# Attention and FFN on one core: the order of two kinds of exp on ScalarE, of the logs on VectorE, and of PSUM evictions

## The chip, the cores and the metric

The kernel runs on one core of a Trainium2 chip. The metric is the device time of one execution in microseconds (us), the median of several runs. A profile is one further execution, recorded by the hardware. The engines are written PE (TensorE, matmul), PEld (its weight loads), DVE (VectorE), ACT (ScalarE), POOL (GpSimd) and SP (SyncE, which issues DMAs). Each engine works through its own queue in order; engines wait for each other through semaphores.

## The reference

Sixteen sequences of 512 rows and 128 columns are layer-normalised. Sixteen causal heads (key width 8, value width 64) and a gated FFN both start from the normalised rows, and both are added to the input:

```python
def _L0_attn_ref(x, Wq, Wk, Wv, Wo):
    HEADS, D_MODEL, D_V = (16, 128, 64)
    ...
    scores = jnp.einsum('bhqd,bhkd->bhqk', q, k) / scale
    scores = jnp.where(causal, jnp.asarray(-jnp.inf, scores.dtype), scores)
    attn = jax.nn.softmax(scores, axis=-1)
    ctx = jnp.einsum('bhqk,bhkd->bhqd', attn, v)
    ...
    return out @ Wo

# FFN: r = sigmoid(xr @ W_r.T); k = square(relu(xk @ W_k.T)); r * (k @ W_v.T)
x = L0_attn_x
xn = _layernorm(x, axis=-1)
x = x + _L0_attn_ref(xn, ...) + _L0_ffn_ref(xn, ...)
```

All of it is in float32.

## The kernel before

**Two passes over the scores.** Every score is computed twice. The first pass is row-major: `rowscores` (L328) writes queries on partitions and keys along the row into a PSUM tile `sm`, `rowmask` (L341) adds the causal mask with four more matmuls, `rowmax` (L359) takes the negated row maximum on DVE into `negm`, and `rowsum` (L378) runs an exp on ACT, in place, one per head and block, whose accumulator is the row's sum. An ACT exp with an accumulator is two instructions in the trace: the ACTIVATE and an ACTIVATION_READ_ACCUMULATOR behind it; the end of the second is what others wait for. From maximum and sum, `log_sums` (L389, a Ln on ACT) and `sub_logs` (L394, one small subtraction on DVE) make minus the maximum minus the log of the sum, `turn_stats` (L398) transposes it on PE into a tile `pm` and copies it out in two halves on DVE (`mh`, `ml`), and `put_stats` (L409) writes it by DMA from POOL as two more rows of the query operand. The second pass is key-major: `scores` (L424) writes keys on partitions into a PSUM tile `sT`; because of the added rows these scores are already normalised, and `weights` (L435) takes one exp of 128x1024 from `sT` into `e`, the attention weights, and zeroes the triangle on POOL. `weigh` (L447) multiplies `e` by the values into `av`, `take_ctx` (L462) evicts `av` on DVE, `project_out` (L468) does the last product into `po`.

**Units.** Two head pairs of one sequence make a group of five units, so that a sequence (a batch in the code) has 20 units and the whole run 320. This text calls the place of a unit in its group its kind, 0 to 4, and its place in the sequence its position, 0 to 19. `ROWS` and `KEYS` (L301 to L315) say what a unit holds: `rowsum` has four exps in kinds 0, 2 (384, 384, 128 and 128 columns) and 4 (four of 256), and two of 512 in kinds 1 and 3. `weights` is one exp of 128x1024 in each.

**What sets the order.** Nothing is scheduled automatically: the wrapper `_InOrder` (L33) keeps every engine's queue in the order in which the Python code issues, so all instructions carry its line, 42, in the trace, and are told apart by their tiles. `unit_work(n)` (L531) issues one step of a software pipeline: row scores, mask and maximum for unit n+11, row exps for unit n+10 (`LEAD`), key-major scores and weights for unit n. Per engine, one step is therefore:

- PE: row scores of n+11, key-major scores of n, mask of n+11, then the pieces (projections, FFN) and `weigh`; in a step of kind 1 `weigh` comes ahead of the pieces. In a step of kind 0 the transpose `pm` comes last.
- ACT: the row exps of n+10, in kind 4 the Ln, then the key-major exp of n, then the FFN's exp in position 1.
- DVE: in kinds 0 and 2 `take_ctx`, then `rowmax`, then the pieces' evictions. In kind 0 `sub_logs` is the last piece, and the two small copies of `pm` follow.

**Buffers.** `sm` has two PSUM buffers, so the row scores of n+11 go where those of n+9 were, and PE waits for the last accumulator read of `rowsum` in step n-1. `sT` has one buffer, so the key-major scores of step n wait for the key-major exp of step n-1. `av` has one. All small products (`pv`, `pr`, `pq`, `pk`, `pkv`, `po`, `pm`) share one PSUM tile `m` once the pipeline runs (`m_tile`, L150), so each waits until DVE has evicted the one before. `at(n, ...)` (L492) puts pieces on a step; L504 to L507 place `ffn_sig` (a reciprocal of 128x128 on DVE) and `project_v` (a product and its eviction); both fall on positions 13 and 18 (in the first sequence 13, 14 and 18).

Of the kernel before, what the change touches and what calls it, by code (L numbers as in the profile page):

```python
# [12 lines left out]
AF = mybir.ActivationFunctionType  # L13
# [4 lines left out]
P = 128  # L18
# [29 lines left out]
def attn_ffn_kernel(  # L48
# [48 lines left out]
    pe, dve, act = _InOrder(tc, nc.tensor), _InOrder(tc, nc.vector), _InOrder(tc, nc.scalar)  # L97
# [11 lines left out]
    for name, w in (("wq", Wq), ("wk", Wk)):  # L109
        t = one.tile([P, H * DK], FP, tag=f"{name}_n", name=f"{name}_n")  # L110
# [5 lines left out]
    for i, w in enumerate((W_r, W_k, W_v)):  # L116
        t = one.tile([P, D], FP, tag=f"ffn_n{i}", name=f"ffn_n{i}")
# [172 lines left out]
    def ffn_out(b):  # L290
# [10 lines left out]
    ROWS = (  # L301
        ((0, 2, 0), (0, 0, 384)),
        ((0, 3, 0),),
        ((1, 2, 0), (1, 0, 384)),
        ((1, 3, 0),),
        ((0, 1, 0), (1, 1, 256)),
    )
# [11 lines left out]
    def unit_of(n):  # L319

        n, t = divmod(n, UNITS)
        b, g = divmod(n, NPAIR // 2)
        return (b, g, t) if 0 <= b < B else None
# [4 lines left out]
    def rowscores(b, g, t):  # L328
        q, k = qs[b % 2], ks[b % 2]
        sm = sms[b, g, t] = ps_sm.tile([P, 2, 512], FP, tag="sm", name=f"sm_{b}_{g}_{t}")  # L330
        for w, i, to in ROWS[t]:
            n = (i + 1) * P
            for u in range(2):
                s = slice(64 * u, 64 * u + RS)

                pe.matmul(
                    sm[:, u, to : to + n], q[s, 2 * g + w, i * P : n], k[s, 2 * g + w, :n],
                    start=(to == 0), stop=False,
                )

    def rowmask(b, g, t):  # L341

        ends = [to + (i + 1) * P for _, i, to in ROWS[t]]
        step = ends[-1] - ends[0] or P
        for c in range(2):
            for u in range(2):
                s = slice(64 * u, 64 * u + 64)
                cols = sms[b, g, t][:, u, ends[0] - P :]
                if len(ends) > 1 and step > P:
                    cols = cols.rearrange("q (m k) -> q m k", k=P)[:, 0 :: step // P, 64 * c :]  # L350
                else:
                    cols = cols.rearrange("q (m k) -> q m k", k=P)[:, :, 64 * c :]
                pe.matmul(
                    cols, id64[s, c, :],
                    mask64[s, c : c + 1, 64 * c :].to_broadcast([64, len(ends), P - 64 * c]),
                    start=False, stop=(c == 1),
                )
# [17 lines left out]
                negm[:, :, w, i], sm[:, :, to : to + (i + 1) * P], AX.X, ALU.max, negate=True  # L375
            )

    def rowsum(b, g, t):  # L378
        negm, z = stats[b, g]
        sm = sms.pop((b, g, t))  # L380
        for w, i, to in ROWS[t]:
            for u in range(2):
                cols = sm[:, u, to : to + (i + 1) * P]
                act.activation(
                    cols, cols, AF.Exp,
                    bias=negm[:, u, w, i : i + 1], accum_out=z[:, u, w, i : i + 1],
                )

    def log_sums(b, g):  # L389
        lz = stat.tile([P, 2, 2, NB], FP, tag="lz", name=f"lz_{b}_{g}")  # L390
# [3 lines left out]
    def sub_logs(b, g):  # L394
        negm, z, lz = stats[b, g]
        dve.tensor_tensor(lz, negm, lz, ALU.subtract)
# [12 lines left out]
    def put_stats(b, g):  # L409

        for n, half in enumerate(stats.pop((b, g))):
            for u in range(2):
                r = 64 * u + RS + n
                pool.dma_start(
                    out=qs[b % 2].bitcast(FP)[r : r + 1, 2 * g : 2 * g + 2, :].rearrange(
                        "o p (i t) -> o (p i) t", t=P
                    ),
                    in_=half.bitcast(FP)[2 * NB * u : 2 * NB * u + 2 * NB],
                )
# [4 lines left out]
    def scores(b, g, t):  # L424
        q, k = qs[b % 2], ks[b % 2]
        st = sts[b, g, t] = ps_st.tile([P, 2, 512], FP, tag="sT", name=f"sT_{b}_{g}_{t}")
        for w, j, to in KEYS[t]:
            for u in range(2):
                s = slice(64 * u, 64 * u + RA)
                pe.matmul(  # L430
                    st[:, u, to : to + T - j * P], k[s, 2 * g + w, j * P : (j + 1) * P],
                    q[s, 2 * g + w, j * P : T], start=(to == 0), stop=(to + T - j * P == 512),
                )

    def weights(b, g, t):  # L435
        e = ep.tile([P, 2, 512], FP, tag="e", name=f"e_{b}_{g}_{t}")
        act.activation(e, sts.pop((b, g, t)), AF.Exp)
        for w, j, to in KEYS[t]:

            diag = e[:, :, to : to + P]  # L440
            pool.affine_select(
                out=diag, in_=diag, compare_op=ALU.is_ge, fill=0.0, base=0,
                pattern=[[0, 2], [1, P]], channel_multiplier=-1,
            )
            es[b, 2 * g + w, j] = e[:, :, to : to + T - j * P]
# [16 lines left out]
    def take_ctx(b, p):  # L462
        c = ctxp.tile([P, T], FP, tag="ctx", name=f"ctx_{b}_{p}")
        dve.tensor_copy(c, avs.pop((b, p)))
        ctxs[b, p] = c
# [21 lines left out]

    todo, turns, puts = {}, {}, {}  # L490

    def at(n, f, *args):  # L492
        todo.setdefault(n, []).append((f, args))
# [4 lines left out]
    for b in range(B):  # L498
        n0 = b * per
        if b + 1 < B:  # L500
            r = 0 if b else 7
            at(n0 + r, ffn_r, b + 1)
            at(n0 + r + 1, ffn_exp, b + 1)
            for c, n in enumerate((3, 8, 13, 18) if b else (11, 13, 14, 18)):  # L504
                at(n0 + n, ffn_sig, b + 1, c)
            for m, n in enumerate((1 if b else 3, 5, 12, 13, 14, 16, 17, 18)):
                at(n0 + n, project_v, b + 1, m // 2, m % 2)  # L507
            at(n0 + 7, mix_prev, b + 1, 1)
            at(n0 + 9, mix, b + 1, 1)
            at(n0 + 11, ffn_k, b + 1)  # L510
            at(n0 + 19, ffn_out, b + 1)
            for m, n in enumerate((-1, -1, 0, 0, 4, 4, 5, 5) if b else (0, 0, 0, 0, 4, 4, 5, 5)):
                at(n0 + n, spread_qk, b + 1, *SPREAD[m], slice(0, NPAIR // 2))
            for m, n in enumerate((8, 9, 9, 10, 10, 14, 14, 15)):
                at(n0 + n, spread_qk, b + 1, *SPREAD[m], slice(NPAIR // 2, NPAIR))
        if b + 2 < B:
            at(n0 + 4, deviation, b + 2)
            for c in range(NB):
                at(n0 + (1, 1, 3, 3)[c], row_moments, b + 2, c)
                at(n0 + 4 + c // 2, normalise, b + 2, c)  # L520
            at(n0 + 6, transpose_xn, b + 2)
            at(n0 + 10, project_qk, b + 2, False)
            at(n0 + 15, project_qk, b + 2, True)
            at(n0 + 12, mix_prev, b + 2, 0)
            at(n0 + 14, mix, b + 2, 0)
        for p, n in enumerate((2, 3, 3, 4, 7, 8, 8, 9) if b < B - 1 else (-8, -7, -7, -6, -3, -2, 0, 3)):
            at(n0 + per + n, project_out, b, p)
        if b + 3 < B:
            at(n0 + 11, load_x, b + 3)

    def unit_work(n):  # L531
        now, stat_now, stat_next = (unit_of(n + m) for m in (0, LEAD, LEAD + 1))
        if n in puts:
            put_stats(*puts.pop(n))

        if stat_next:
            rowscores(*stat_next)
        if now:
            scores(*now)
        if stat_next:  # L540
            rowmask(*stat_next)
        t = n % UNITS
        done = {0: (n - UNITS, 0), 2: (n - UNITS, 1)}.get(t)
        if done and unit_of(done[0]):
            b, g, _ = unit_of(done[0])
            take_ctx(b, 2 * g + done[1])
        if stat_next:
            rowmax(*stat_next)

        if stat_now:  # L550
            rowsum(*stat_now)
            b, g, kind = stat_now
            if kind == UNITS - 1:
                log_sums(b, g)
                at(n + 1, sub_logs, b, g)
                turns[n + 1] = puts[n + 2] = b, g
        if now:
            weights(*now)
        pieces = todo.pop(n, ())
        if t != 1:  # L560
            for f, args in pieces:
                f(*args)
        since, w, blocks = WEIGHED[t]
        if unit_of(n - since):
            b, g, _ = unit_of(n - since)
            for j in blocks:
                weigh(b, 2 * g + w, j, (t, j) in ((1, 3), (4, 3)))
        if t == 1:
            for f, args in pieces:
                f(*args)  # L570
        if n in turns:
            turn_stats(*turns.pop(n))
# [41 lines left out]
    for u in range(2):  # L614
        half = slice(64 * u, 64 * u + 64)
        for c in range(2):
            cols = slice(64 * c, 64 * c + 64)
# [81 lines left out]
```

## Time and profile before

| what | value |
|---|---|
| median of three runs | 1032.33 us (1031.92 to 1036.72) |
| the profiled execution, its own time | 1032.25 us |
| its span, first to last instruction | 1030.5 us |
| PE busy | 961.6 us (93%) |
| PE weight loads busy | 525.6 us (51%) |
| ACT busy | 923.9 us (90%) |
| DVE busy | 792.8 us (77%) |
| POOL busy | 520.3 us (50%) |
| row exps, 1024 of them, and their accumulator reads | 513.1 + 201.1 us |
| key-major exps, 320 | 324.3 us |
| mean granted PE clock | 0.979 |

The profiled execution lies 0.08 us under the median, so its rows can be read as the median's. Between about 61 us and 980 us the run repeats a sequence's 20 units about every 60.7 us; before lies the loading and the first ten units' row statistics, behind it the last units' key-major work.

How to read the views quoted below. The page's busy line gives busy microseconds, share of the span and number of instructions of each engine. The chain of waits is the work that ended last, followed back to what released it. A line of a stretch gives, after its start and end, its length and each engine's busy time, then the granted PE clock, the DMA share and GB/s. A line of the waits names who waited for whom, then the total in us, the number of times and the longest. A line of the timeline gives start and length in us, the engine, the operation, output and input tile, shapes and count, and in brackets the idle time ahead of it and who ended that.

### The profile page before, as it was taken

The numbers are of one execution on the slowest core, as the hardware profiler recorded it, in microseconds if no ns is written. First come the engines' busy times: TensorE is split into PE (matmuls) and PEld (weight loads), VectorE is DVE, ScalarE is ACT, GpSimd is POOL, SyncE is SP. The second block draws the span as 40 slices with busy tenths as digits, with TensorE's granted clock in tenths as the row PEclk, the third lists the DMA queues.
The fourth block names the chain that finished last, engine by engine and source line by source line (L and its number), as shares of the span: only waits on it lengthen the run. The fifth ranks groups of instructions, "written<-read, shape, count | busy, mean of one in ns | idle before, by whom it ended". The sixth has DMA issues, their size and how long they took to land.

```text
span 1030.5 us, 24120 instructions
## 1 busy us (share of the span) xinstructions
PE 961.6 (93%) x8771; PEld 525.6 (51%) x8771; DVE 792.8 (77%) x1316; ACT 923.9 (90%) x2449; POOL 520.3 (50%) x957
## 2 busy tenths in 40 slices
PE   3888999999999999999999999999999999999997
PEld 1334454545546464554645555464555646455454
DVE  4877878787787878788788877878878787877741
ACT  0788999999999999999999999999999999999982
POOL 4156454644646464464655546464464546444432
PEclk8679999999999999999999999999999999999999
DMA  7811515225250532625053252504425140433000
GB/s 193 147 23 44 104 25 104 32 67 90 54 104 10 108 42 53 105 54 99 8 109 49 54 105 53 94 14 100 57 54 95 34 97 4 98 49 49 3 13 11
DMA packets 59973, 67.19 MB, mean 65 GB/s; under 512 B 12928, under 2 KB 33024, under 8 KB 59856
## 3 DMA queue, kind: packets, MB, share of 16 engines
q1 hardware_dynamic: 48688, 61.89, 32.1%
q0 software_dynamic: 8640, 1.34, 1.0%
q10 hardware_dynamic: 2528, 2.43, 0.8%
q8 instruction: 70, 1.15, 0.5%
q14 instruction: 47, 0.39, 0.2%
HBM read 39.13 MB, written 25.17 MB: 62 GB/s over the span
## 4 chain that ended last, share of the span: by engine, by line
PE 57%; ACT 19%; DVE 17%; issue 6%; POOL 1%; DMA 0%; ACTq 0%; DVEq 0%; POOLq 0%
PE av L42 16%; ACT sm L42 13%; PE sm L42 12%; PE po L42 10%; DVE negm L42 7%; PE sT L42 7%; ACT e L42 6%; PE pv L42 6%; DVE sig L42 2%; PE pr L42 1%; DVE v L42 1%; PE pm L42 1%; PE pkv L42 1%; DVE xmix L42 1%; PE xnTp L42 1%
## 5 line engine op out<-in xcount | busy, mean ns | idle before, releaser
L42 ACT ACTIVATE sm<-sm,negm 128x384 f32<-128x384 f32 (+3 forms) x1024 | 513.1, 501 | 71.9 <-DMA q<-qh 25.4
L42 DVE TENSOR_REDUCE negm<-sm 128x2 f32<-128x768 f32 (+3 forms) x448 | 398.9, 915 | 125.4 <-PE sm L42 125.1
L42 POOL TENSOR_SCALAR_AFFINE_SELECT e<-e 128x256 f32<-128x256 f32 x512 | 208.2, 426 | 418.2 <-ACT e L42 416.0
L42 ACT ACTIVATE e<-sT 128x1024 f32<-128x1024 f32 x320 | 324.3, 1013 | 21.7 <-PE sT L42 21.7
L42 PE MATMUL av<-e,v 128*64 128x512 f32 (+3 forms) x2048 | 336.2, 439 | 1.3 <-POOL e L42 0.7
L42 PEld LDWEIGHTS av<-e,v 128*64 128x64 f32 x2048 | 138.1, 137 | 166.5 <-issue 139.2
L42 ACT ACTIVATION_READ_ACCUMULATOR sm<-sm,negm 128x1 f32 x1024 | 201.1, 196 | 0.0
L42 PE MATMUL sm<-k,q 33*128 33x384 f32 (+3 forms) x1024 | 163.7, 377 | 4.3 <-ACT sm L42 4.3
L42 PEld LDWEIGHTS sm<-k,q 33*128 33x128 f32 x1024 | 82.9, 188 | 149.0 <-ACT sm L42 72.7
L42 PE MATMUL sT<-q,k 35*128 35x512 f32 (+3 forms) x1024 | 146.5, 338 | 4.5 <-ACT e L42 4.3
L42 PE MATMUL pv<-wv,xnT 128*64 128x512 f32 x512 | 141.5, 632 | 6.9 <-DVE v L42 5.3
L42 PE MATMUL po<-wo,ctx 128*64 128x128 f32 x2048 | 133.2, 277 | 2.1 <-DVE ctx L42 1.6
L42 PEld LDWEIGHTS po<-wo,ctx 128*64 128x64 f32 x2048 | 109.8, 137 | 17.1 <-issue 9.7
L42 PEld LDWEIGHTS sT<-q,k 35*128 35x128 f32 x1024 | 90.2, 187 | 28.6 <-ACT e L42 22.6
L42 PE MATMUL sm<-mask,id 64*128 64x128 bf16 (+2 forms) x1280 | 103.0, 236 | 0.0
L42 DVE COPY v<-pv 128x512 f32<-128x512 f32 x128 | 85.9, 671 | 19.0 <-PE pv L42 18.9
L42 DVE COPY ctx<-av 128x512 f32<-128x512 f32 x128 | 87.3, 682 | 15.6 <-PE av L42 15.5
L42 POOL DMA_DIRECT2D q<-mh x128 | 69.8, 548 | 48.7 <-DVE mh L42 40.7
L42 POOL DMA_DIRECT2D q<-ml x128 | 65.9, 519 | 0.3 <-issue 0.3
L42 DVE RECIPROCAL sig<-e_sig 128x128 f32<-128x128 f32 x64 | 60.2, 941 | 0.0
L42 POOL TENSOR_SCALAR prev<-xnT,omm 128x512 f32<-128x512 f32 x32 | 50.0, 1563 | 12.8 <-DVE xmix L42 12.8
L42 PEld LDWEIGHTS <-id 64*128 64x128 bf16 x1280 | 40.1, 97 | 29.6 <-issue 15.7
(65 smaller groups left out, 568.4 us busy)
## 6 DMA issues: line engine op xcount, KB each, us to landing
q<-q SPq DMA_DIRECT2D x124, 128.0 KB, 4.9
k<-k SPq DMA_DIRECT2D x124, 128.0 KB, 5.5
k<-kh SPq DMA_DIRECT2D x30, 256.0 KB, 2.6
x<-in_L_attn_x_dram SPq DMA_DIRECT2D x16, 256.0 KB, 3.2
q<-qh SPq DMA_DIRECT2D x16, 256.0 KB, 4.2
q<-ql SPq DMA_DIRECT2D x16, 256.0 KB, 4.1
out_dram<-o SPq DMA_DIRECT2D x16, 256.0 KB, 2.8
k<-kl SPq DMA_DIRECT2D x15, 256.0 KB, 2.0
```

The source lines that it names most:

```text
L42: return self._tc.keep_in_program_order(f(*args, **kwargs))
```

## The change

Three orders change; no instruction is added or taken away.

- `rowsum` takes a function and calls it ahead of its last exp. `unit_work` hands it `weights` of the step. On ACT the key-major exp of each step thereby stands in front of the last row exp, and in kind 4 the Ln stands behind both.
- `sub_logs` is no longer the last piece of a step of kind 0: it is issued ahead of `take_ctx` and `rowmax`.
- `project_v` is entered ahead of `ffn_sig`, so that where both fall on one step the eviction of `pv` stands ahead of the reciprocal on DVE. On PE the order of products does not change.

```diff
-    def rowsum(b, g, t):
+    def rowsum(between, b, g, t):
         negm, z = stats[b, g]
         sm = sms.pop((b, g, t))
-        for w, i, to in ROWS[t]:
-            for u in range(2):
-                cols = sm[:, u, to : to + (i + 1) * P]
-                act.activation(
-                    cols, cols, AF.Exp,
-                    bias=negm[:, u, w, i : i + 1], accum_out=z[:, u, w, i : i + 1],
-                )
+        blocks = [(u, *block) for block in ROWS[t] for u in range(2)]
+        for m, (u, w, i, to) in enumerate(blocks):
+            if m == len(blocks) - 1:
+                between()
+            cols = sm[:, u, to : to + (i + 1) * P]
+            act.activation(
+                cols, cols, AF.Exp,
+                bias=negm[:, u, w, i : i + 1], accum_out=z[:, u, w, i : i + 1],
+            )
...
+            for m, n in enumerate((1 if b else 3, 5, 12, 13, 14, 16, 17, 18)):
+                at(n0 + n, project_v, b + 1, m // 2, m % 2)
             for c, n in enumerate((3, 8, 13, 18) if b else (11, 13, 14, 18)):
                 at(n0 + n, ffn_sig, b + 1, c)
-            for m, n in enumerate((1 if b else 3, 5, 12, 13, 14, 16, 17, 18)):
-                at(n0 + n, project_v, b + 1, m // 2, m % 2)
...
         if stat_next:
             rowmask(*stat_next)
+        if n in subs:
+            sub_logs(*subs.pop(n))
...
-        if stat_now:
-            rowsum(*stat_now)
+        attend = (lambda: weights(*now)) if now else lambda: None
+        if not stat_now:
+            attend()
+        else:
+            rowsum(attend, *stat_now)
             b, g, kind = stat_now
             if kind == UNITS - 1:
                 log_sums(b, g)
-                at(n + 1, sub_logs, b, g)
-                turns[n + 1] = puts[n + 2] = b, g
-        if now:
-            weights(*now)
+                subs[n + 1] = turns[n + 1] = puts[n + 2] = b, g
```

More of the change, by code (lines that the diff above doesn't have):

```diff
@@ L484, in project_out @@
             sp.dma_start(out=out[b].rearrange("(c p) d -> p c d", p=P), in_=o)
-    todo, turns, puts = {}, {}, {}
+    todo, subs, turns, puts = {}, {}, {}, {}
     def at(n, f, *args):
```

## The prediction

> **What bounds the kernel now.** First the page: the busy line and the engine shares of the chain.
>
> ```profile
> PE 961.6 (93%) x8771; PEld 525.6 (51%) x8771; DVE 792.8 (77%) x1316; ACT 923.9 (90%) x2449; POOL 520.3 (50%) x957
> ...
> PE 57%; ACT 19%; DVE 17%; issue 6%; POOL 1%; DMA 0%; ACTq 0%; DVEq 0%; POOLq 0%
> ```
>
> Two engines are nearly full and the chain hands over between them. Next, one sequence of 20 units from the middle of the run, as a stretch:
>
> ```profile
> 616.90:677.60 60.70, 58.45 (x550) 32.40 (x552) 49.02 (x81) 57.51 (x154) 32.46 (x60) 1.00 0.37 68
> ```
>
> Of 60.70 us PE is busy 58.45 and ACT 57.51, at full clock. Neither has more than 3.2 us to give, so what counts is who waits for whom inside a unit. The waits over the whole run:
>
> ```profile
> PE pm L42 <- DVE lz L42: 24.5, 31, 2.0
> ...
> PEld sT L42 <- ACT e L42: 22.6, 65, 1.0
> ACT e L42 <- PE sT L42: 21.7, 28, 1.9
> ACT sm L42 <- DVE negm L42: 20.0, 37, 1.7
> ```
>
> All four touch the change. The timeline of positions 10 to 14 shows where they sit, PE first, then ACT:
>
> ```profile
> 640.77 0.27 PE L42 MATMUL pm<-ident,lz 128*16 128x128 f32 x1 [0.92 <-DVE lz L42]
> 640.97 0.50 PE L42 MATMUL sm<-k,q 33*128 33x384 f32 x4
> 641.31 0.45 PE L42 MATMUL sT<-q,k 35*128 35x256 f32 x4
> ...
> 643.74 0.50 PE L42 MATMUL sm<-k,q 33*128 33x512 f32 x2
> ...
> 646.47 0.51 PE L42 MATMUL sm<-k,q 33*128 33x256 f32 x4
> ...
> 650.12 1.08 PE L42 MATMUL pv<-wv,xnT 128*64 128x512 f32 x4 [0.34 <-DVE v L42]
> ```
>
> ```profile
> 641.86 1.02 ACT L42 ACTIVATE e<-sT 128x1024 f32<-128x1024 f32 x1 [0.48 <-PE sT L42]
> 643.37 0.56 ACT L42 ACTIVATE sm<-sm,negm 128x384 f32<-128x384 f32 x1 [0.48 <-DVE negm L42]
> ...
> 645.26 0.34 ACT L42 ACTIVATE sm<-sm,negm 128x128 f32<-128x128 f32 x1
> 645.53 0.19 ACT L42 ACTIVATION_READ_ACCUMULATOR sm<-sm,negm 128x1 f32 x1
> 645.62 1.01 ACT L42 ACTIVATE e<-sT 128x1024 f32<-128x1024 f32 x1
> 646.52 0.66 ACT L42 ACTIVATE sm<-sm,negm 128x512 f32<-128x512 f32 x1
> ```
>
> PE comes 0.92 us late into position 11 because `pm` waits; ACT then waits for `sT` and once more for a row maximum. Elsewhere PE starts a unit between 0.35 us before and 0.7 us after ACT does. I write S for the start of a unit's row scores on PE and measure PE by the time from S to S. Read so, that sequence gives (position: us) kind 0: 0: 3.60, 5: 3.35, 10: 4.25, 15: 4.18; kind 1: 1: 2.77, 6: 2.50, 11: 2.77, 16: 2.78; kind 2: 2: 2.95, 7: 2.74, 12 and 17: 2.73; kind 3: 3: 3.33, 8: 3.42, 13: 2.29, 18: 2.30; kind 4: 4 and 9: 2.79, 14: 3.23, 19: 3.24. Sum 60.74.
>
> **ACT's own time falls.** A row exp behind a row exp starts 0.03 us after the accumulator read (one ends at 645.23, the next exp starts at 645.26); the key-major exp starts 0.09 us ahead of that read's end (645.53 + 0.19 against 645.62), and a row exp 0.11 us ahead of the key-major exp's end (646.63 against 646.52). Before, one gap of the first sort precedes the last row exp; after, the last row exp stands behind the key-major exp. The trace has no such pair within one unit; its ends are the two rows just named, and I take the overlap, since in the built program that exp's wait counts the accumulator read before the key-major exp, which has long passed. A first row exp straight behind a read occurs in the lead-in and overlaps too (read 48.13 to 48.32, exp at 48.22). So each unit costs ACT 0.13 us less: 41 us over 310 units, if ACT alone set the time.
>
> The Trainium skill, page "Perfetto Trace Analysis", section "Identifying the Most-Contended Engine", says not to take matmul busy time for PE's headroom but the weight loads' share, and to work on the engine of highest occupancy. By that rule PE stands at 51%, ACT at 90% is the engine to relieve, and the sum would be 1032 - 41 = 991. The row of the stretch speaks against it: between the waits named, PE's queue has no gap to give.
>
> **What PE gains.** Before, the key-major scores wait for the key-major exp of the unit before, the last thing on ACT: at positions 3, 8, 0 and 15 they begin 0.39 to 0.50 us after S where 0.34 is the rule, and start cold, which costs 0.10 more. After, that exp has ended before S is possible. Without wait and cold start positions 3 and 8 fall to 3.18 (3.42 - 0.14 - 0.10) and 0 to the 3.35 that 5 has: -0.15, -0.24, -0.25. At 14 and 19 the eviction of `pv` no longer stands behind the 0.94 us reciprocal; PE's wait there (0.34 and 0.36) goes, but see below.
>
> **The logs first.** `pm` shares its PSUM tile with the product ahead of it, so at positions 10 and 15 it must also wait for that product's second copy (`ql`, `kl`), which DVE makes right before the old place of `sub_logs`. DVE is without a gap there, so moving the subtraction's 0.09 us to the front only swaps the two. What is left is the shorter hand-over (0.06 us from copy to PE at 650.12, 0.14 from `lz` to `pm`): -0.07 at 10. At 15 also the earlier mask counts; I take -0.15. At 0 and 5 `pm` does not wait. `sub_logs` now waits for a Ln that ends some 1.0 us later; behind it stand `take_ctx` and the row maximum. The Ln ends 0.09 us after ACT's unit and PE's scores and mask need 0.83 us from S, so I cost this at nothing; its cover is the 0.57 to 1.08 us by which the row maximum for kind 1 is early. POOL's triangles follow the key-major exp and come earlier with it; the DMAs of `put_stats` follow `pm`, and the scores that need them are four units off. Both cost nothing.
>
> **What PE loses.** Row scores of the next unit need the last accumulator read, now the end of ACT's whole unit. PE follows such a read by 0.05 us (read end 83.94, start 83.99). From S in kind 1: `sT` ends at +0.79, the exp starts 0.10 later (641.76 to 641.86), the last row exp 0.90 later, its read ends 0.77 later, PE 0.05: 2.61. PE's own work exceeds that at positions 1, 11 and 16; at 6 it costs 2.61 - 2.50 = +0.11. Kind 2 next: its first row exp starts at 0.79 + 0.10 + 0.90 + 0.67 = 2.46 after kind 1's S; then 0.70 + 0.70 + 0.36 + 0.90 + 0.46 + 0.05 = 3.17, so kind 3 cannot start before 5.63. That leaves kind 2 2.86 at 12 and 17 (+0.13 each), 3.02 at 7 (+0.28), and at 2, where the FFN's exp adds 0.52 on ACT, 3.38 (+0.43). Kind 3, short of PE work at 13 and 18: `sT` ends at +0.74, exp 0.04 later (the spacing in the few stalled units of this kind), 0.90, 0.77, 0.05: 2.50, +0.20 each. Kind 4 behind them: ACT begins 0.15 before S and needs 0.60 + 0.60 + 0.46 + 0.90 + 0.56, PE 0.05: 3.02, so of the 3.23 only 0.21 is won, at 14 and 19.
>
> **Sum for a sequence.** Gains: 0.15 + 0.24 + 0.25 + 0.07 + 0.15 + 0.21 + 0.21 = 1.28. Losses: 0.11 + 0.13 + 0.13 + 0.28 + 0.43 + 0.20 + 0.20 = 1.48. Net +0.20, over some 15 sequences (the last has little PE work; its ACT units come to 14.45 per group against 14.49) +3 us. The profiled execution took 1032.25, the median is 1032.33: **1035 us**, +0.3%.
>
> **Rivals.**
>
> - *The last row exp doesn't overlap the key-major exp* (slower). Then 0.13 us comes back wherever ACT paces PE: in kind 1 and kind 2 of each group, and at 13, 14, 18, 19: 12 times, 1.56 per sequence, +23 on the forecast: 1058. It decides from about 0.03 us per unit on. For it: each row exp behind a row exp shows the gap. Against: 48.22 and 646.52.
> - *DVE is held by the later Ln* (slower). Logs, `take_ctx` and row maximum shift by up to the 1.0 us that the Ln moves; beyond the smallest cover of 0.57 that is 0.4 in each of four groups, 1.6 per sequence, 24 at most: 1059; half of it 1047. For it: the 20.0 us that ACT waits for row maxima already. Against: the cover.
> - *PE comes late anyway* (faster). If PE reaches its row scores after the last read more often than I count, losses shrink and gains stay: without any loss 1.28 x 15 = 19, that is 1013; with half the losses, 0.54 x 15 = 8: 1024.
> - *The reordering changes nothing*: waits only change names, 1032.
>
> **How the numbers follow.** About 0.5% (5 us) is what a measurement of this kernel can tell from no change. Forecast 0.55, own range 1029 to 1041, of it 0.18 above 1037.5; no overlap 0.11; held DVE 0.08; late PE 0.17, of it 0.15 below 1027.2; nothing 0.09. Slower 0.18 + 0.11 + 0.08 = 0.37; faster 0.15; within 0.5% 0.37 + 0.02 + 0.09 = 0.48. The range leaves out the full prices of the rivals and keeps their halves: 1022 to 1050.
>
> **What would show it.** Right: PE's wait of `sT` for `e` gone, a new wait of `sm` for ACT's last `sm` of 0.1 to 0.5 us in kinds 2 and 3, ACT waiting for `sT` in kind 1 of every group and in kind 3, `pm` still waiting at positions 10 and 15, a sequence of about 60.9. Wrong: row exps starting behind the key-major exp's end, `negm` waits grown in kind 1, or a sequence away from 60.6 to 61.3.

## The result and the profile after

The changed kernel takes 1037.66 us (median of 12 runs, 1034.72 to 1040.47). The kernel before took 1032.88 us in the runs beside it (1031.1 to 1036.84). The ratio is 1.0045, 95% interval 1.0033 to 1.0057: slower by a little under the 0.5% that was called no change, and 2.7 us over the forecast of 1035. The profiled execution of the changed kernel took 1035.95 us, its span is 1034.2 us.

The page of the changed kernel, busy line and engine shares of the chain of waits:

```profile
PE 945.0 (91%) x8771; PEld 517.9 (50%) x8771; DVE 791.3 (77%) x1316; ACT 897.8 (87%) x2449; POOL 517.0 (50%) x957
...
ACT 36%; PE 36%; DVE 18%; issue 7%; DMA 1%; POOL 1%; ACTq 0%; SPq 0%; POOLq 0%
```

ACT has 26 us less to do and the run is longer. In the chain ACT's share went from 19% to 36%, and PE's from 57% to 36%.

One sequence of the changed kernel, as a stretch (start and end, length, busy time of PE, PEld, DVE, ACT and POOL, granted clock, DMA share, GB/s):

```profile
607.80:669.00 61.20, 57.82 (x548) 32.01 (x548) 49.04 (x81) 55.85 (x154) 32.31 (x60) 1.00 0.36 67
```

A sequence grew from 60.73 to 61.21 us (sums of the medians by position). PE now leaves 3.4 us of it unused and ACT 5.4, so both wait more than they did. The waits of the changed kernel say for what:

```profile
PEld sm L42 <- ACT sm L42: 171.6, 228, 3.1
...
ACT e L42 <- PE sT L42: 79.9, 135, 2.4
...
PE sm L42 <- ACT sm L42: 31.2, 88, 1.5
...
PE pm L42 <- DVE kl L42: 12.5, 14, 0.9
PE pm L42 <- DVE ql L42: 12.4, 14, 0.9
...
ACT sm L42 <- DVE negm L42: 4.4, 5, 1.4
...
PEld sT L42 <- ACT e L42: 2.8, 5, 0.8
```

Four waits have changed places. The key-major scores no longer wait for the key-major exp (22.6 us before, 2.8 now). PE's row scores now wait for ACT's last accumulator read, 88 times for 31.2 us. ACT waits for the key-major scores 135 times, 79.9 us, where it was 28 times and 21.7 us. The transpose `pm` waits as long as before, but for the second copies `ql` and `kl`.

The timeline of the changed kernel, positions 11 to 14, PE and then ACT:

```profile
642.19 0.27 PE L42 MATMUL pm<-ident,lz 128*16 128x128 f32 x1 [0.92 <-DVE ql L42]
642.38 0.50 PE L42 MATMUL sm<-k,q 33*128 33x384 f32 x4
642.72 0.46 PE L42 MATMUL sT<-q,k 35*128 35x256 f32 x4
...
645.16 0.50 PE L42 MATMUL sm<-k,q 33*128 33x512 f32 x2
...
648.04 0.50 PE L42 MATMUL sm<-k,q 33*128 33x256 f32 x4
648.38 0.39 PE L42 MATMUL sT<-q,k 35*128 35x512 f32 x2
...
650.56 0.50 PE L42 MATMUL sm<-k,q 33*128 33x384 f32 x4 [0.17 <-ACT sm L42]
```

```profile
643.28 1.02 ACT L42 ACTIVATE e<-sT 128x1024 f32<-128x1024 f32 x1 [1.62 <-PE sT L42]
644.20 0.66 ACT L42 ACTIVATE sm<-sm,negm 128x512 f32<-128x512 f32 x1
...
647.53 0.34 ACT L42 ACTIVATE sm<-sm,negm 128x128 f32<-128x128 f32 x1
647.78 0.21 ACT L42 ACTIVATION_READ_ACCUMULATOR sm<-sm,negm 128x1 f32 x1
...
648.82 1.02 ACT L42 ACTIVATE e<-sT 128x1024 f32<-128x1024 f32 x1 [0.16 <-PE sT L42]
649.74 0.66 ACT L42 ACTIVATE sm<-sm,negm 128x512 f32<-128x512 f32 x1
650.31 0.20 ACT L42 ACTIVATION_READ_ACCUMULATOR sm<-sm,negm 128x1 f32 x1
```

On DVE, the second copy of the queries, which `pm` at 642.19 waits for:

```profile
641.35 0.69 DVE L42 TENSOR_TENSOR ql<-pq,qh 128x512 fp32r<-128x512 f32 x1
```

Two things are to be seen. The last row exp starts before the key-major exp ends: 649.74 against 648.82 + 1.02 = 649.84. So it does overlap. And the two engines now hand over in a ring. A read ends at 647.99 and PE's row scores start at 648.04. The key-major scores behind them end at 648.77, and the key-major exp starts at 648.82 after a wait. The row exp and its read end at 650.51, and the next row scores start at 650.56. In a unit of kind 3 (648.04 to 650.56) that ring alone sets the time: 2.52 us, where PE's own work took 2.29.

From S to S, in us, for the positions that were to move, and 5:

| position | before | forecast | after |
|---|---|---|---|
| 0 | 3.60 | 3.35 | 3.29 |
| 2 | 2.95 | 3.38 | 3.40 |
| 3, 8 | 3.33, 3.42 | 3.18, 3.18 | 3.18, 3.17 |
| 5 | 3.35 | 3.35 | 3.28 |
| 6 | 2.50 | 2.61 | 2.64 |
| 7 | 2.74 | 3.02 | 3.02 |
| 10 | 4.25 | 4.18 | 4.26 |
| 12, 17 | 2.73 | 2.86 | 2.88 |
| 13, 18 | 2.29 | 2.50 | 2.52 |
| 14, 19 | 3.23, 3.24 | 3.02 | 3.02 |
| 15 | 4.18 | 4.03 | 4.23 |

All but two came within 0.07 us of the forecast. Positions 10 and 15 did not move as forecast, and they hold the question for the experiments: +0.01 and +0.05 instead of -0.07 and -0.15.

The profiled spans add up as follows. The second sequence starts at 120.62 before and at 118.08 after (-2.54). From there to the start of the last sequence 14 sequences take 849.01 and 855.16 us (+6.15); the rest takes 60.90 and 61.00. Together +3.7, as the spans say. The first term can't be put down to the change: in the first experiment below, which differs from the changed kernel only in the order on DVE, the second sequence starts at 122.69.

### The profile page after: what moved, and what is told of

Same layout as the page of the kernel before. It is cut to its first block, busy times and chain, and to the rows that moved or that the text cites. A ratio compares the mean times of both kernels' runs of the same rounds, so it can differ in the third digit from the quotient of the medians.

```text
span 1034.2 us, 24119 instructions
## 1 busy us (share of the span) xinstructions
PE 945.0 (91%) x8771; PEld 517.9 (50%) x8771; DVE 791.3 (77%) x1316; ACT 897.8 (87%) x2449; POOL 517.0 (50%) x957
## 4 chain that ended last, share of the span: by engine, by line
ACT 36%; PE 36%; DVE 18%; issue 7%; DMA 1%; POOL 1%; ACTq 0%; SPq 0%; POOLq 0%
ACT sm L42 20%; ACT e L42 15%; PE sm L42 10%; PE av L42 7%; PE po L42 7%; DVE negm L42 7%; PE sT L42 5%; DVE v L42 2%; DVE xmix L42 2%; PE pv L42 2%; PE pr L42 1%; PE pm L42 1%; DVE sig L42 1%; DVE kl L42 1%; DVE kh L42 1%
## 5 line engine op out<-in xcount | busy, mean ns | idle before, releaser
L42 POOL TENSOR_SCALAR_AFFINE_SELECT e<-e 128x256 f32<-128x256 f32 x512 | 205.5, 421 | 388.9 <-ACT e L42 388.7
L42 ACT ACTIVATE e<-sT 128x1024 f32<-128x1024 f32 x320 | 325.9, 1019 | 80.1 <-PE sT L42 79.9
L42 ACT ACTIVATION_READ_ACCUMULATOR sm<-sm,negm 128x1 f32 x1024 | 206.1, 201 | 0.0
L42 PE MATMUL sm<-k,q 33*128 33x384 f32 (+3 forms) x1024 | 164.6, 376 | 36.1 <-ACT sm L42 31.2
L42 PEld LDWEIGHTS sm<-k,q 33*128 33x128 f32 x1024 | 83.9, 187 | 189.1 <-ACT sm L42 171.6
L42 PE MATMUL pv<-wv,xnT 128*64 128x512 f32 x512 | 138.8, 621 | 1.3 <-DVE ffn L42 0.3
L42 PE MATMUL sT<-q,k 35*128 35x512 f32 (+3 forms) x1024 | 137.5, 322 | 1.3 <-DMA q<-ml 1.0
```

What stands on the lines that cost most here:

```text
L42: return self._tc.keep_in_program_order(f(*args, **kwargs))
```

## The experiments

The theory was that of the prediction: the new ACT order takes time off ACT that PE can't use, since PE's row scores now wait for the end of ACT's whole unit; the logs first and the evictions first give back a little. The rivals were that DVE, held by the later Ln, is what costs, and that the parts act in another mixture. Three runs do one part alone, one undoes the costly half of a part, three look for what would let the new order pay, and three test what the first seven left open.

**The ACT order alone.** From the changed kernel, the logs and the evictions are put back:

```diff
+            for c, n in enumerate((3, 8, 13, 18) if b else (11, 13, 14, 18)):
+                at(n0 + n, ffn_sig, b + 1, c)
             for m, n in enumerate((1 if b else 3, 5, 12, 13, 14, 16, 17, 18)):
                 at(n0 + n, project_v, b + 1, m // 2, m % 2)
-            for c, n in enumerate((3, 8, 13, 18) if b else (11, 13, 14, 18)):
-                at(n0 + n, ffn_sig, b + 1, c)
...
-        if n in subs:
-            sub_logs(*subs.pop(n))
...
-                subs[n + 1] = turns[n + 1] = puts[n + 2] = b, g
+                at(n + 1, sub_logs, b, g)
+                turns[n + 1] = puts[n + 2] = b, g
```

> Only the order on ACT is changed: the key-major exp in front of the last row exp, and the Ln behind both; logs and evictions as in the kernel before. Gate theory: PE's row scores now wait for the end of ACT's whole unit. Working the sequence of 20 units through with the durations of the profile before, a sequence takes 61.2 to 61.3 us instead of 60.73, so the run is 7 to 9 us slower than before: 1039 to 1042, more than the full change, since the two other parts' gains are missing. Rival, held DVE: the cost of the change lies in the subtraction that waits for the later Ln; with the subtraction back at its late place this kernel should then be no slower than before, 1030 to 1034. Rival, ACT's own 0.13 us per unit wins: 1000 to 1028.

Measured: 1040.11 us (1038.54 to 1043.17), ratio 1.0068 [1.0049, 1.0087]. A sequence takes 61.18 us. All gains and losses at positions 0, 2, 3, 6 to 8, 12 to 14 and 17 to 19 are those of the whole change, within 0.01 us. So the ACT order makes nearly the whole result. The subtraction stands at its old place here, so DVE isn't held by it, and the loss is there: that rival falls. Two positions differ: 15 takes 4.06 here, 0.12 less than before, and 5 takes 3.44, 0.09 more. In the changed kernel they take 4.23 and 3.28, so on top of the ACT order the logs first lose at 15 what they win at 5. The medians lie 2.45 us apart, the sequences only 0.03; that difference stays open.

**The logs first alone.** The kernel before, with only `sub_logs` moved:

```diff
+        if n in subs:
+            sub_logs(*subs.pop(n))
...
-                at(n + 1, sub_logs, b, g)
-                turns[n + 1] = puts[n + 2] = b, g
+                subs[n + 1] = turns[n + 1] = puts[n + 2] = b, g
```

> Only the subtraction of the logs is moved to the front of VectorE's unit. Gate theory with the shared PSUM tile: at positions 10 and 15 the transpose waits for the second copy of the product ahead of it in the same PSUM tile, so the wait only changes its name from lz to ql and kl; a sequence is 0.07 to 0.2 us shorter, the run 1 to 3 us faster: 1029 to 1032. Rival: the wait of 24.5 us of the transpose for lz is the subtraction's own place in the queue and goes: 10 to 22 us faster, 1010 to 1022.

Measured: 1033.64 us (1032.26 to 1035.06), ratio 1.0004 [0.999, 1.0017]. No difference that can be told, and far from the rival. But the theory is missed too, in sign: a sequence takes 60.99 us, 0.26 more than before, where 0.07 to 0.2 less was expected. Position 15 falls from 4.18 to 4.10, but 5 grows from 3.35 to 3.49 and 10 from 4.25 to 4.46. What is special about 5 and 10 was seen only later, with the eighth run.

**The evictions first alone.** The kernel before, with the two loops swapped:

```diff
-            for c, n in enumerate((3, 8, 13, 18) if b else (11, 13, 14, 18)):
-                at(n0 + n, ffn_sig, b + 1, c)
             for m, n in enumerate((1 if b else 3, 5, 12, 13, 14, 16, 17, 18)):
                 at(n0 + n, project_v, b + 1, m // 2, m % 2)
+            for c, n in enumerate((3, 8, 13, 18) if b else (11, 13, 14, 18)):
+                at(n0 + n, ffn_sig, b + 1, c)
```

> Only the eviction of the value projection ahead of the reciprocal, at positions 13 and 18. PE's waits of 0.34 and 0.36 us for that eviction at positions 14 and 19 go, but ACT is behind PE there, so PE then waits for ACT's key-major exp instead: 0 to 0.1 us per sequence, the run 0 to 2 us faster: 1030 to 1033. Rival: PE's queue sets the time also there, 0.70 us per sequence, 10 us faster: 1022.

Measured: 1033.85 us (1030.69 to 1037.27), ratio 1.0013 [0.9996, 1.003]: no difference that can be told, 0.85 us above the range of the theory. PE's wait for `v` goes, and positions 14 and 19 fall by 0.42 each, to 2.81 and 2.82. The next two, 15 and 0, rise by the same 0.42, to 4.60 and 4.02: in the old order PE then waits for ACT's key-major exp instead. In the changed kernel that wait is gone, and positions 14 and 19 take 3.02. But they take 3.02 in the first experiment as well, where the evictions stand at their old place. So the ACT order alone brings this gain, and the evictions first add nothing to it there.

**The key-major exp last again where a unit has two row exps (kinds 1 and 3).**

```diff
-            if m == len(blocks) - 1:
+            if m == len(blocks) - 1 and len(blocks) > 2:
                 between()
...
+        if len(blocks) == 2:
+            between()
```

> The full change, but in units of kinds 1 and 3 (two row exps of 512) the key-major exp stays behind both, as before; only kinds 0, 2 and 4 (four row exps) have the new order. Gate theory: the gate bites where only one row exp of 0.67 us covers PE's 0.8 us of row and key-major scores, that is in kinds 1 and 3; without them a sequence takes 60.3 us instead of 61.2, the run 8 to 14 us faster than the full change and 4 to 7 us faster than before: 1025 to 1029. Rival, ACT's 0.13 us per unit is what the change gives and the loss is elsewhere (DVE): two fifths of that gain are lost, 5 us slower than the full change, about 1042.

Measured: 1025.69 us (1024.1 to 1029.71), ratio 0.9936 [0.9915, 0.9958], a sequence 60.58 us. So 12 us of the changed kernel's time come from kinds 1 and 3 by the medians, 9.5 by the sequences (0.63 each). Position 13 is back at 2.28, 18 at 2.30, and 2 falls from 3.40 to 3.13; a part is lost again at 15, which rises from 4.23 to 4.35, and at 14 and 19, from 3.02 to 3.13 and 3.12. The reading is that in kinds 1 and 3 ACT has a single row exp to run before it needs the key-major scores, too little to cover the time until they come; the next run puts it to the test.

**PE issues the key-major scores first.** If the ring is what costs, the key-major scores should not stand behind the row scores that close it. The changed kernel, with PE's two score steps swapped:

```diff
+        if now:
+            scores(*now)
         if stat_next:
             rowscores(*stat_next)
-        if now:
-            scores(*now)
```

> The full change, and in PE's queue the key-major scores of a unit stand ahead of the next unit's row scores. Gate theory: the key-major scores need only the key-major exp of the unit before, which now ends before ACT's last row exp; so they start while that row exp runs, and the key-major exp finds them done. The 0.2 to 0.45 us per unit of PE's wait in kinds 2 and 3 and ACT's wait for them in kind 1 go; a sequence worked through in this order takes about 59.3 us, the run 18 to 24 us faster than before: 1009 to 1015. Rival: the loss is ACT's or DVE's, not the gate's; then the order on PE matters little and the run stays within 3 us of the full change, 1035 to 1041. A second rival: the row scores, now 0.34 us later, delay the row maxima, and kinds 0 and 2 wait for those: 1040 to 1050.

Measured: 1009.62 us (1009.02 to 1012.55), ratio 0.9781 [0.9765, 0.9798], as expected. Its waits:

```profile
PEld sT L42 <- ACT sm L42: 63.0, 120, 1.1
PEld sT L42 <- ACT e L42: 62.9, 105, 1.5
ACT e L42 <- PE sT L42: 47.8, 43, 1.8
...
PEld sm L42 <- ACT sm L42: 19.6, 55, 3.1
...
PE pm L42 <- DVE kl L42: 13.2, 14, 0.9
PE pm L42 <- DVE ql L42: 12.7, 14, 0.9
```

ACT's waits for `sT` fell from 135 to 43, weight loads for row scores wait 19.6 us for ACT instead of 171.6, and positions 2, 6, 7, 12, 13, 17 and 18 are back at what they took in the kernel before, or 0.05 under it, to within 0.01. Not every position gains: 14 and 19 fall by 0.25 and 0.23 against the changed kernel, and 15 rises from 4.23 to 4.69. `pm` waits about as long as before, 25.9 us in all; that is the next edit.

**The projections of queries and keys off the steps of the transpose.** The changed kernel, with these two projections moved from positions 10 and 15 to 13 and 18. To make room, two projections of values go from 13 and 18 to 10 and 15, and two reciprocals from 13 and 18 to 3 and 8:

```diff
-            for m, n in enumerate((1 if b else 3, 5, 12, 13, 14, 16, 17, 18)):
+            for m, n in enumerate((1 if b else 3, 5, 10, 12, 14, 15, 16, 17)):
                 at(n0 + n, project_v, b + 1, m // 2, m % 2)
-            for c, n in enumerate((3, 8, 13, 18) if b else (11, 13, 14, 18)):
+            for c, n in enumerate((3, 3, 8, 8) if b else (11, 13, 14, 18)):
                 at(n0 + n, ffn_sig, b + 1, c)
...
-            at(n0 + 10, project_qk, b + 2, False)
-            at(n0 + 15, project_qk, b + 2, True)
+            at(n0 + 13, project_qk, b + 2, False)
+            at(n0 + 18, project_qk, b + 2, True)
```

> The full change, with the query and key projections moved from positions 10 and 15 (kind 0) to 13 and 18 (kind 3), two value projections moved from there to 10 and 15, and the reciprocals of those positions moved to 3 and 8. Shared tile theory: the transpose at 10 and 15 waits because the product ahead of it in the one PSUM tile needs two copies on DVE; with one copy the wait of 0.9 us at each falls to near nothing. A sequence takes 59.6 to 60.0 us instead of 61.2, the run 17 to 24 us faster than the full change: 1013 to 1020. Rival: that wait is not what the sequence's length hangs on, ACT being behind PE anyway: 1033 to 1039.

Measured: 1017.22 us (1016.87 to 1020.16), ratio 0.9849 [0.9836, 0.9862], as expected. At positions 10 and 15 a product with one eviction now stands ahead of `pm`, not one with two copies: 4.26 falls to 3.45 and 4.23 to 3.46, and no other position grows by more than 0.01.

**Both together.**

> Both of the edits above together: key-major scores first on PE, and the query and key projections at 13 and 18. If the two waits are separate, their gains add: a sequence of about 58.1 to 58.5 us, the run at 990 to 1000. If one hides the other, the run stays near the better of the two, 1009 to 1015.

Measured: 993.35 us (992.63 to 994.36), ratio 0.9619 [0.9606, 0.9632]. This is the best version: 39 us less than the kernel before and 44 less than the changed one. Its stretch:

```profile
583.71:642.04 58.33, 57.37 (x550) 32.00 (x548) 49.10 (x82) 55.78 (x154) 31.87 (x60) 1.00 0.35 70
```

PE is busy 57.37 of 58.33 us. ACT's busy time is what it is in the changed kernel (55.78 against 55.85): the ACT time was there to be used, and PE's order and `pm` stood in the way.

**What holds the subtraction at position 15?** The changed kernel's timeline around it, with both DVE and POOL (S is 653.58):

```profile
653.14 1.25 POOL L42 TENSOR_SCALAR_AFFINE_SELECT e<-e 128x256 f32<-128x256 f32 x2 [2.74 <-ACT e L42]
...
653.38 0.74 DVE L42 SCALAR_TENSOR_TENSOR xmix<-xnT,mus,prev 128x512 f32<-128x512 f32 x1
...
654.03 0.38 DVE L42 TENSOR_TENSOR lz<-negm,lz 128x16 f32<-128x16 f32 x1
...
654.34 0.68 DVE L42 COPY ctx<-av 128x512 f32<-128x512 f32 x1
...
654.94 1.21 DVE L42 TENSOR_REDUCE negm<-sm 128x2 f32<-128x1024 f32 x1
```

POOL's row holds two triangles. A window that begins at 653.6 shows the second by itself:

```profile
653.50 0.89 POOL L42 TENSOR_SCALAR_AFFINE_SELECT e<-e 128x256 f32<-128x256 f32 x1
```

The subtraction takes 0.38 us where 0.17 is usual, and ends at 654.41, just after this triangle at 654.39. No wait is named; it has started and doesn't finish. The triangle started 0.53 us ahead of it (the 0.89 of the expectation below counts from the first of the two), and it is long itself: 0.89 us where 0.41 is usual, beside `xmix` on DVE, which had started 0.12 us ahead of it. The row maximum behind it starts 1.36 us after S, though the mask ended 0.84 after S (654.16 + 0.26). The test moves the subtraction behind `take_ctx`, at this position alone:

```diff
-        if n in subs:
+        if n in subs and n % 20 != 15:
             sub_logs(*subs.pop(n))
...
             take_ctx(b, 2 * g + done[1])
+        if n in subs:
+            sub_logs(*subs.pop(n))
         if stat_next:
             rowmax(*stat_next)
```

> The changed kernel with one edit: at position 15 alone `sub_logs` is issued behind `take_ctx` and ahead of `rowmax`. Theory: in the changed kernel the subtraction of position 15 takes 0.37 us (0.17 at positions 0, 5 and 10) and ends 0.02 us behind a triangle on POOL that started 0.89 us ahead of it, so POOL holds it. Behind the eviction of `av`, 0.60 us later, that triangle has ended: the subtraction takes 0.17 and the row maximum starts 0.2 us earlier, the copies `kh` and `kl` and the transpose with it; position 15 falls from 4.23 to 4.00-4.06 us, a sequence from 61.21 to 61.0, and the time by 3 us against the changed kernel, to 1033-1036 us. Rival one: the subtraction is long at this position whatever POOL does; it stays at 0.37 us and position 15 at 4.2: 1037-1039. Rival two: something other than DVE's row sets position 15; the subtraction is short and position 15 stays at 4.2: 1037-1039.

Measured: 1034.5 us (1032.74 to 1036.0), ratio 1.0014 [1.0004, 1.0025], 3.2 us under the changed kernel, and position 15 at 4.02. Both rivals fall: the subtraction is short at its new place, and the position is shorter by the same 0.21 us. The same rows of this kernel, where S is 653.95 and the row maximum starts 1.14 us after it:

```profile
653.75 0.74 DVE L42 SCALAR_TENSOR_TENSOR xmix<-xnT,mus,prev 128x512 f32<-128x512 f32 x1
654.41 0.68 DVE L42 COPY ctx<-av 128x512 f32<-128x512 f32 x1
655.01 0.17 DVE L42 TENSOR_TENSOR lz<-negm,lz 128x16 f32<-128x16 f32 x1
655.09 1.22 DVE L42 TENSOR_REDUCE negm<-sm 128x2 f32<-128x1024 f32 x1
```

Taken over all 64 subtractions (busy us and mean ns; idle before them), first the changed kernel, then this one, then the logs first alone:

```profile
L42 DVE TENSOR_TENSOR lz<-negm,lz 128x16 f32<-128x16 f32 x64 | 13.6, 212 | 5.5 <-ACT lz L42 5.5
```

```profile
L42 DVE TENSOR_TENSOR lz<-negm,lz 128x16 f32<-128x16 f32 x64 | 11.0, 171 | 5.1 <-ACT lz L42 5.1
```

```profile
L42 DVE TENSOR_TENSOR lz<-negm,lz 128x16 f32<-128x16 f32 x64 | 17.3, 271 | 0.5 <-ACT lz L42 0.5
```

That explains the second run too. With the logs first alone the subtraction takes 0.38 us at positions 5 and 10 and mostly 0.17 at 15, and just 5 and 10 had grown. There it runs beside a triangle that had started 0.07 and 0.60 us ahead of it; both times it ends 0.02 to 0.03 us after that triangle. Taken over the twelve traces of this text, 96 subtractions start 0.027 us or more after a triangle that still has 0.15 us or more to run: every one ends 0.02 to 0.03 us after it. Another 37 start within 0.02 us of a triangle, and none of these is held.

The Trainium skill, page "SBUF — State Buffer", section "Who interferes with whom", states that a VectorE instruction with two SBUF inputs contends with a GpSimd instruction that reads SBUF, that the ports they share are an exclusive lock, and that the order of issue decides which of the two blocks. Both operands of the subtraction are in SBUF, and the rows beside triangles agree with this. Beside other work on POOL less is lost: at position 5 of the first experiment the subtraction starts 0.20 us behind the POOL instruction that writes `xn`, takes 0.25 us and ends 0.32 us ahead of that one's end. Why it isn't held to the end there stays open.

**Key-major scores first without the change.** The same swap on PE as in the fifth run, in the kernel before.

> The kernel before with one edit: on PE the key-major scores of a unit ahead of the row scores of the next (the edit that took 28 us off the changed kernel). Theory: it pays only where the key-major exp doesn't end ACT's unit. In the old order that exp is ACT's last of each unit, and with one buffer of `sT` the key-major scores must wait for it; now the row scores stand behind this wait as well. Worked out unit by unit with the trace's durations, a sequence takes 61.2 us against 60.7: 6 us slower than before, 1035-1042 us, with a wait of `sT` for `e` in most units. Rival: key-major scores ahead pay in either order of ACT, since they let the key-major exp start earlier: 1010-1023 us.

Measured: 1043.11 us (1042.51 to 1048.24), ratio 1.0111 [1.009, 1.0132]: slower, as the theory has it, and 1 us beyond its range. A sequence takes 61.53 us. The profiled execution took 1048.24 us, 5 more than the median, and most of that lies ahead of the second sequence, which starts at 126.24. Its waits have this line, against 62.9 us in the fifth run:

```profile
PEld sT L42 <- ACT e L42: 116.4, 169, 2.3
```

In the old order the key-major exp ends ACT's unit, and the swap makes the row scores wait for it too. The swap that takes 28 us off the changed kernel adds 10 us to the one before.

**Both edits without the change.** The kernel before, with the swap and the moved projections.

> The kernel before (old order of the exps, of the logs and of the evictions) with both edits that brought the changed kernel to 993 us: key-major scores ahead of row scores on PE, and the projections of queries and keys off the steps of the transpose. Theory: the orders of the change are what the other edits need; worked out unit by unit a sequence takes 60.0 us against 58.3 with the change: 1016-1026 us. Rival: the change is worth a loss of 0.4% here as it is alone: 987-992 us.

Measured: 1029.45 us (1026.87 to 1032.88), ratio 0.9967 [0.9953, 0.9981]. The rival falls; the theory's range is missed by 3 us on the other side, so the change is worth more here than was worked out: 36 us against the same two edits with it. A sequence takes 60.37 us, 2.03 more than with the change. Which of the change's three orders carries how much of these 2.03 wasn't taken apart.

## Why the prediction was right, and where it was not

The forecast of 1035 us and no change that can be told was right in its main mechanism and its sign. In size the parts were close, but their net is a small difference between large terms: +0.48 us a sequence where +0.20 was worked out, more than twice as much. That the run got only 4.8 us longer where +3 was forecast is in part luck: 15 sequences of +0.48 would be 7.2 us, and 1040. The parts, by its own steps:

- **ACT's own time falls**: right. The last row exp starts 0.10 us ahead of the key-major exp's end, and ACT's busy time fell by 26.1 us. The rival without overlap is refuted by the same row.
- **What PE gains**: right in size, in part for another reason. The forecast gains at 0, 3, 8, 14 and 19 add to 1.06; measured were 1.14, and 0.07 at position 5 that wasn't counted. At 0, 3 and 8 the cold start and the wait of `sT` went as costed. At 14 and 19 the 0.21 was put down to the eviction of `pv` ahead of the reciprocal; the first experiment wins it without that (3.02 at both), so there it came from the order on ACT.
- **What PE loses**: right, a little too small. The forecast said 1.48 and the runs showed 1.63, each position 0.02 to 0.03 more except 7, which came out exact. The chain "read, row scores, key-major scores, key-major exp, last row exp, read" is what was counted, and the timeline at 648.04 shows it link by link.
- **The logs first**: this step failed. It gave -0.07 at position 10 and -0.15 at 15; +0.01 and +0.05 came. This 0.28 is the size of the whole error of the sum; the two terms above cancel. Two parts were wrong. At 10 the hand-over to `pm` was taken as 0.06 us, from the row of another product; from `ql` it takes 0.15 (642.04 to 642.19), no less than the 0.14 from `lz` that it replaces. And "POOL's triangles follow the key-major exp and come earlier with it ... cost nothing" was wrong at 15: they come early enough to lie under the subtraction at its new place and hold it for 0.21 us. The eighth run takes just that away, and position 15 falls to 4.02, where 4.03 was forecast.
- **Held DVE**: refuted as a cost. ACT's waits for row maxima fell from 20.0 to 4.4 us. DVE waits 5.5 us in all for the later Ln.
- **PE comes late anyway**: refuted. The losses came in full, at every position named.
- **The rule of the most-contended engine**: the sum by it was 991. ACT, the busiest engine by that reading, lost 26 us of busy time and the kernel got 5 us slower, so the rule as the prediction read it misled here. (The section it cites names one more measure for PE beside the weight loads' share, MFU, the share of the peak arithmetic; no run here gives it.) The row of the stretch, which had PE busy 58.45 of 60.70 us, decided rightly. That 993 was reached later, with two further edits on PE's side, does not make the rule right for this change.

The medians moved by 4.8 us and the sequences' sum by 0.48 x 15 = 7.2. What lies between was not settled; in the two profiles it is the 2.54 us by which the second sequence starts earlier. The start of the second sequence moves by several us between profiled kernels for reasons that no run here took apart.

## What to carry to other kernels

Where two engines are both nearly full, count the ring of hand-overs between them unit by unit, not the busy time of either: an order that saves one engine 26 us can cost the pair 5, and the same change is worth 33 us once the other engine's order fits it (1043.11 against 1009.62, the ninth and the fifth run), 36 with the projections moved as well. When a small instruction is moved, look at what else runs at its new place, on other engines too, and not only at what it waits for; a length of 0.38 us where 0.17 is usual, without a wait named ahead of it, is the sign. Take a hand-over from the row of the same pair of instructions, not from a neighbour.

## What the runs showed of the hardware that was not expected

- A 128x16 subtraction on DVE with both operands in SBUF takes 0.16 to 0.18 us alone and up to 0.40 beside a POOL triangle that started 0.03 us or more ahead of it, and ends 0.02 to 0.03 us after it. Where the triangle ends within 0.1 us of the subtraction's start and POOL begins its next product after that start (position 0 of the changed kernel), it takes 0.17 to 0.18. Holds can follow one another: at position 15 the triangle that holds the subtraction takes 0.89 us where 0.41 is usual, beside a DVE instruction that started ahead of it.
- The first start of a sequence moved by several us between profiled kernels that hardly differ: row scores of unit 11 start at 51.73 us in the changed kernel and at 54.36 in that of the eighth run, whose edit touches a single subtraction up to there. The rows of the third unit, ahead of it, are 0.57 us apart already (29.84 and 30.41). So 2 us between two single profiles say nothing of such an edit. The times from S to S do: at position 15 the 13 sequences read lie between 4.23 and 4.24 in the one and between 4.02 and 4.03 in the other.
